# A recommender's history gather: one tile of rows in 256 moved from GpSimd to SyncE

## The chip, the cores and the metric

The kernel runs on one core of a Trainium2 chip. The metric is the device time in microseconds of one execution; for the kernel before it is a median of three executions. The engines are named as in the profile: PE (TensorE, matrix multiply), DVE (VectorE), ACT (ScalarE), POOL (GpSimd) and SP (SyncE); "SPq" is SyncE's queue of issued DMAs.

## The reference

A Deep-Interest recommender. Each of B = 16384 users has a history of L = 200 items. Every history item is looked up in an item table of V rows of D = 64 floats, compared with the candidate item, scored by a small network whose activation ("dice") is normalised over the batch, and the weighted rows are summed. Then a small three-layer head gives the output.

```python
u, it, c, h = u_emb[user], i_emb[item], c_emb[cate], i_emb[hist]     # h: (200, 16384, 64)
feat = concatenate([h, itb, h - itb, h * itb], axis=-1)              # itb: it, repeated for each l
a = dice(feat @ au_W1 + au_b1, au_alpha, axis=1)                     # mean, var over the 16384 users
cur = sum((a @ au_W2 + au_b2) * h, axis=0)
z = concatenate([u, it, c, cur], axis=-1)
z = dice(z @ W1 + b1, alpha1, axis=0); z = dice(z @ W2 + b2, alpha2, axis=0)
return z @ W3 + b3
```

So 200 x 16384, some 3.3 million, table rows are looked up by index, and that gather is most of the kernel's traffic.

## The kernel before, in words

**First stage.** The item table is copied to a table of its own in device memory (`table`), each row 2 x 64 floats (512 bytes): the item's embedding and, beside it, its product with the weights that act on the history item alone. SyncE loads blocks (L217), VectorE transposes, TensorE multiplies, ScalarE's queue stores (L232, L234). Meanwhile GpSimd gathers the user, item and category rows (24 groups of 16 gathers). `xi`, in device memory too, keeps for each of 8 chunks of users the product that belongs to the candidate item.

**The main loop.** The 16384 users are 128 partitions x 128 tiles. A *tile* is one row of `table` for each of the 128 partitions; a *step* is 16 tiles (TD), one chunk of one history position; 8 steps (ND) make a history position l, so there are 1600 steps k. A hardware loop (L411) runs 8 passes of 24 positions (192 steps), and the last 8 positions (64 steps) follow unrolled, with 10 steps to drain. The order within a step is written out by hand (`step`, L376), each engine keeps it, and an engine waits where its next instruction's data or buffer is not ready. Steps are pipelined: step k fetches k, turns k-1, ends the hidden layer of k-2 and weighs k-10.

- `fetch(k)` (L306): 16 indirect DMAs by GpSimd, one a tile (`gather`, L135, issue at L138), into `land[k % 12]`, a ring of 12 buffers; and on SyncE the load of `xit[k % 2]` from `xi` (L309).
- `load_hist_ids` (L148): on SyncE, once in 8 steps, the indices of the next history position into one of two `idx` buffers (L149); it waits for the last gather that read that buffer.
- ScalarE: the gate of k-10 (L386, L389), the copy of `xit` into `px` (L391), and, after the turn, `ph` (L393). The copy at L391 frees the `xit` buffer that SyncE waits for.
- VectorE: `turn(k-1)` (four transposes, L317, the first to wait for the gathers of k-1), the hidden layer (L329, L331), `hm` (L323), once in 8 steps the moments of the batch (L359 to L373), and `weigh(k-10)` (L337 to L353). L352 is the last to read `land[(k-10) % 12]`; a gather two steps later writes that buffer again.
- TensorE: `px` from `hm` (L176).

Completion of DMAs is counted on 8 semaphores for SyncE's and ScalarE's queues and 8 for GpSimd's, taken in turn; a DMA waits for the one eight before it. At the end of a loop pass all engines meet and the counts are set back. GpSimd goes into the first pass without waiting for SyncE; there, the ten buffers of `land` for k = -10 to -1 are set to zero by VectorE (L286) and pass through the first steps as if they had been fetched.

Of the kernel before, what the change touches and what calls it, by code (L numbers as in the profile page):

```python
# [8 lines left out]
F32 = mybir.dt.float32  # L9
I32 = mybir.dt.int32  # L10
# [4 lines left out]
P = 128  # L15
D = 64
# [3 lines left out]
CD = 2 * CH  # L20
LPB = 24
LAND = 12
EARLY = 4
IDX = 2
XI = 2
# [3 lines left out]
def din_kernel(  # L29
# [24 lines left out]
    nc = tc.nc  # L54
    L, B = r_hist.shape
    NT = B // P
    TD = 2 * CD // P
    ND = NT // TD
    V = i_emb.shape[0]
# [3 lines left out]
    const = ctx.enter_context(tc.tile_pool(name="const", bufs=1))  # L63
# [7 lines left out]
    def quarter(e, g, n=S):  # L71

        return slice((2 * e + g) * S, (2 * e + g) * S + n)
# [21 lines left out]
    for e in range(2):  # L95
        rows = au_W1.rearrange("(g d) a -> d g a", d=D)[e * S : (e + 1) * S]
        for g in range(2):
            r = quarter(e, g)
            nc.sync.dma_start(au_w[r], rows)
            for q, (a0, n) in enumerate(parts):  # L100
                c, a = quarter(q, g, n), slice(a0, a0 + n)
# [3 lines left out]
    for g in range(2):  # L105
        for q, (a0, n) in enumerate(parts):
            r, a = quarter(q, g, n), slice(a0, a0 + n)
# [12 lines left out]

    land = [const.tile([P, TD, 2 * D], F32, name=f"land{i}") for i in range(EARLY)]
    idx = [const.tile([P, NT], I32, name=f"idx{i}") for i in range(IDX)]
    stats = [const.tile([P, 2 * ND, nc.vector.BN_STATS_DIM], F32, name=f"st{i}") for i in range(2)]
    rstds = [const.tile([P, 1], F32, name=f"rs{i}") for i in range(2)]
    shifts = [const.tile([P, 1], F32, name=f"sh{i}") for i in range(2)]
# [5 lines left out]
    table = dram.tile([V, 2 * D], F32, name="table")  # L131
# [3 lines left out]
    def gather(dst, ids, rows):  # L135

        for n in range(ids.shape[1]):
            nc.gpsimd.indirect_dma_start(  # L138
                out=dst[:, n, :],
                out_offset=None,  # L140
                in_=rows,
                in_offset=bass.IndirectOffsetOnAxis(ap=ids[:, n : n + 1], axis=0),
            )
# [3 lines left out]

    def load_hist_ids(i, l):  # L148
        nc.sync.dma_start(idx[i], r_hist[ds(l, 1), :].rearrange("l (p n) -> p (l n)", n=NT))  # L149

    def by_tile(t, i):

        return t[:, ts(i, CH)].rearrange("p (n t) -> p n t", t=S)

    def transpose(dst, rows, n=TD):

        for i in range(2):
            for e in range(2):
                nc.vector.transpose(  # L159
                    by_tile(dst[ts(e, D)], i)[:, :n], rows[ts(i, D), :n, ts(e, S)]  # L160
                )
# [9 lines left out]
    def layer(dst, pairs, n=CH, onto=False):  # L171

        for i in range(2):
            cols = slice(i * CH, i * CH + n)
            for j, (lhsT, rhs) in enumerate(pairs):
                nc.tensor.matmul(  # L176
                    dst[:, cols], lhsT, rhs[:, cols],
                    start=(j == 0 and not onto), stop=(j == len(pairs) - 1),
                    skip_group_check=onto,
                )  # L180
# [13 lines left out]
    with ExitStack() as start:  # L194
# [41 lines left out]
        def fetch_one(j):  # L236
            c, k = j % ND, j // ND
            gather(land[j % EARLY][:, :, :D], ids[k][:, ts(c, TD)], (i_emb, u_emb, c_emb)[k])

        def keep_one(j):  # L240
            c, k = j % ND, j // ND
            if k == 0:
                transpose(itT[:, c], land[j % EARLY])
                layer(ph, [(blk_i, itT[:, c])])
# [3 lines left out]
            else:  # L248
                t = pre.tile([P, CD], F32, tag="t", name="t")
                transpose(t, land[j % EARLY])  # L250
                nc.scalar.dma_start(ucT[k - 1, c], t)
# [20 lines left out]
    with ExitStack() as main:  # L272
        ring = main.enter_context(tc.tile_pool(name="ring", bufs=1))

        land += [
            ring.tile([P, TD, 2 * D], F32, name=f"land{i}") for i in range(EARLY, LAND)
        ]
# [7 lines left out]
        for k in range(-10, 0):  # L285
            nc.vector.memset(land[k % LAND], 0.0)  # L286
        for t in hx:
# [7 lines left out]
        for i in range(2):  # L295
            nc.vector.memset(rstds[i], 0.0)
            nc.vector.memset(shifts[i], 0.0)
        nc.sync.dma_start(xit[-1 % XI], xi[ND - 1])

        def by_row(t):  # L300
            return t.rearrange("p (n d) -> p n d", d=D)

        def x_of(k):
            return land[k % LAND][:, :, D:]

        def fetch(k):  # L306
            l, c = divmod(k, ND)
            gather(land[k % LAND], idx[l % IDX][:, ts(c, TD)], table)
            nc.sync.dma_start(xit[k % XI], xi[c])  # L309

        def turn(k):

            rows = land[k % LAND].rearrange("p n (s e c) -> p n s e c", s=2, e=2)
            for i in range(2):
                for e in range(2):
                    dst = hx[k % 2][ts(e, D), :, ts(i, CH)]
                    nc.vector.transpose(  # L317
                        dst.rearrange("p s (n t) -> p n s t", t=S), rows[ts(i, D), :, :, e]
                    )

        def product(k):

            nc.vector.tensor_mul(hm, ph, itT[:, k % ND])  # L323
            layer(px[k % 2], [(blk_m, hm)], onto=True)

        def hidden(k):

            l, c = divmod(k, ND)
            nc.vector.tensor_add(x_of(k), by_row(px[k % 2]), by_row(hx[k % 2][:, 1]))  # L329
            for i in range(2):  # L330
                nc.vector.bn_stats(  # L331
                    stats[l % 2][:, 2 * c + i, :], x_of(k)[:, ts(i, TD // 2)]
                )

        def weigh(k):
# [14 lines left out]
            c = k % ND  # L350
            rows = land[k % LAND][:, :, :D]
            nc.vector.tensor_mul(by_row(pg), rows, w.unsqueeze(2).to_broadcast([P, TD, D]))  # L352
            nc.vector.tensor_add(cur[:, ts(c, TD)], by_row(pg), cur[:, ts(c, TD)])  # L353

        def moments(l):

            i = l % 2
            mv = small.tile([P, 2], F32, tag="mv", name="mv")
            nc.vector.bn_aggr(mv, stats[i].rearrange("p c s -> p (c s)"))  # L359
            other = small.tile([P, 2], F32, tag="other", name="other")  # L360
            for q in range(2):
                for g in range(2):
                    nc.vector.tensor_copy(other[quarter(q, g)], mv[quarter(q, 1 - g)])
            total = small.tile([P, 2], F32, tag="total", name="total")
            nc.vector.tensor_add(total, mv, other)
            mean = small.tile([P, 1], F32, tag="mean", name="mean")
            nc.vector.tensor_scalar_mul(mean, total[:, 0:1], 0.5)
            dev = small.tile([P, 1], F32, tag="dev", name="dev")
            nc.vector.tensor_sub(dev, mv[:, 0:1], mean)
            half = small.tile([P, 1], F32, tag="half", name="half")  # L370
            nc.vector.tensor_scalar_mul(half, total[:, 1:2], 0.5)
            var = small.tile([P, 1], F32, tag="var", name="var")
            nc.vector.scalar_tensor_tensor(var, dev, dev, half, ALU.mult, ALU.add)  # L373
            scale_and_shift(mean, var, P, rstds[i], shifts[i])

        def step(k, last=None):  # L376


            def has(j):
                return last is None or j <= last  # L380

            if has(k):
                fetch(k)
            if has(k - 10):
                i = (k - 10) // ND % 2
                nc.scalar.activation(  # L386
                    by_row(gate), x_of(k - 10), AF.Sigmoid, bias=shifts[i], scale=rstds[i]
                )
                nc.scalar.activation(pg, gate, AF.Identity, bias=au_al, scale=au_1al)  # L389
            if has(k - 1):  # L390
                nc.scalar.copy(px[(k - 1) % 2], xit[(k - 1) % XI])  # L391
                turn(k - 1)
                nc.scalar.copy(ph, hx[(k - 1) % 2][:, 0])  # L393
            if has(k - 2):
                hidden(k - 2)
            if has(k - 1):
                product(k - 1)
            if has(k - 2) and (k - 2) % ND == ND - 1:
                moments((k - 2) // ND)
            if has(k - 10):  # L400
                weigh(k - 10)

        def steps(l0, n, last):

            for k in range(n * ND + (10 if last else 0)):
                l, c = divmod(k, ND)
                if c == 0 and l + 1 < n + (not last):
                    load_hist_ids((l + 1) % IDX, l0 + l + 1)
                step(k, last=n * ND - 1 if last else None)

        with tc.For_i(0, L - L % LPB, LPB) as l0:  # L411
            with tc.manual_schedule():
# [5 lines left out]
    with ExitStack() as head:  # L418
# [5 lines left out]
        for g in range(2):  # L424
            t = fin.tile([P, 4, Z1], F32, name=f"w1{g}")
# [16 lines left out]
        for i, (v, n) in enumerate(((alpha1, Z1), (alpha2, Z2))):  # L442
            t = fin.tile([n, 1], F32, name=f"al{i}")
# [17 lines left out]
        for c in range(ND):  # L461
            rows = land[c % EARLY].rearrange("p (s n) d -> p s (n d)", s=2)
            for i in range(2):
# [21 lines left out]
        for m in range(2 * ND):  # L485
            a = work.tile([Z1, CD], F32, tag="a1", name="a1")
# [6 lines left out]
        for c in range(ND):  # L493
            a = work.tile([Z2, TD, 2, 2, S], F32, tag="a2", name="a2")
            for g in range(2):
                p, zm = (
                    t.rearrange("z (i n t) -> z i n t", i=2, t=S)
                    for t in dice(1, Z2, 2 * c + g, rstd, shift)
                )
# [38 lines left out]
```

## Time and profile before

| | us |
|---|---|
| median of 3 executions | 32900.87 |
| lowest, highest | 32900.82, 32961.82 |
| the profiled execution | 32903.59 |
| its span on the core | 32901.7 |
| first gather of `table` starts | 489.43 |
| second loop pass, first gather | 4338.58 |
| GpSimd busy with gathers of `table` (25600) | 24157.7 |
| VectorE busy | 25564.2 |
| ScalarE busy | 7641.4 |
| SyncE waiting for ScalarE's copy at L391 | 22516.9 |

A group of instructions is told as line, engine, operation, what is written and read, how many, then busy us and mean ns of one, then the idle time of its engine just before them and what ended most of it. "issue" is idle time in which the engine waited for nothing that the profile shows. Issuing a DMA isn't counted as busy time, but a gather on GpSimd, which is a piece of work for it, is. Times within the execution count from the start of the span.

### The profile page before, as it was taken

The numbers are of one execution on the slowest core, as the hardware profiler recorded it, in microseconds if no ns is written. First come the engines' busy times: TensorE is split into PE (matmuls) and PEld (weight loads), VectorE is DVE, ScalarE is ACT, GpSimd is POOL, SyncE is SP. The second block draws the span as 40 slices with busy tenths as digits, with TensorE's granted clock in tenths as the row PEclk, the third lists the DMA queues.
The fourth block names the chain that finished last, engine by engine and source line by source line (L and its number), as shares of the span: only waits on it lengthen the run. The fifth ranks groups of instructions, "written<-read, shape, count | busy, mean of one in ns | idle before, by whom it ended". The sixth has DMA issues, their size and how long they took to land. (4 is left out here: it accounts for less than half of the span.)

```text
span 32901.7 us, 99907 instructions
## 1 busy us (share of the span) xinstructions
PE 6388.8 (19%) x7216; PEld 2043.0 (6%) x7216; DVE 25564.2 (78%) x28837; ACT 7641.4 (23%) x7113; POOL 24520.4 (75%) x25988
## 2 busy tenths in 40 slices
PE   3111111111111111111111111111111111111113
PEld 0000000000000000000000000000000000000001
DVE  7777777777777777777777777777777777777776
ACT  1222222222222222222222222222222222222222
POOL 7777777777777777777777777777777777777774
PEclk6555555555555555555555555555555555555555
DMA  5222222222222222222222222222222222222221
GB/s 158 79 79 79 79 79 79 79 80 78 80 79 79 79 78 80 79 79 80 78 79 79 80 79 79 80 79 79 79 79 80 79 80 78 79 80 79 80 79 53
DMA packets 1208006, 2648.96 MB, mean 81 GB/s; under 512 B 549078, under 2 KB 575222, under 8 KB 1201142
## 3 DMA queue, kind: packets, MB, share of 16 engines
q0 software_dynamic: 831488, 1691.97, 19.8%
q1 hardware_dynamic: 365238, 887.18, 8.5%
q10 hardware_dynamic: 10560, 63.79, 0.5%
q14 instruction: 705, 5.78, 0.1%
q8 instruction: 15, 0.25, 0.0%
HBM read 2577.24 MB, written 63.91 MB: 80 GB/s over the span
## 5 line engine op out<-in xcount | busy, mean ns | idle before, releaser
L138 POOL DMA_INDIRECT land<-table,idx x25600 | 24157.7, 944 | 7880.7 <-issue 7560.7
L317 DVE STREAM_TRANSPOSE hx<-land 64x1024 f32<-64x1024 f32 x6404 | 7935.6, 1239 | 6418.2 <-DMA land<-table,idx 6265.7
L176 PE MATMUL px<-hm,blk_m 128*128 128x512 f32 x6404 | 5973.2, 1088 | 26045.0 <-DVE hm L323 26045.0
L389 ACT ACTIVATE pg<-gate,au_al,au_1al 128x1024 f32<-128x1024 f32 x1610 | 1943.8, 1207 | 12855.1 <-DVE cur L353 12854.8
L393 ACT COPY ph<-hx 128x1024 f32<-128x1024 f32 x1601 | 1627.7, 1017 | 10702.8 <-DVE hx L317 10702.8
L176 PEld LDWEIGHTS px<-hm,blk_m 128*128 128x128 f32 x6404 | 1878.9, 324 | 30138.6 <-DVE hm L323 28484.2
L331 DVE BATCH_NORM_STATS2 st<-land 128x6 f32<-128x512 f32 x3204 | 2060.6, 685 | 55.0
L338 DVE STREAM_TRANSPOSE yT<-pg 128x1024 f32<-128x1024 f32 x1610 | 2011.6, 1249 | 55.2
L352 DVE TENSOR_TENSOR pg<-land,ph 128x1024 f32<-128x1024 f32 x1610 | 1978.6, 1229 | 54.9
L353 DVE TENSOR_TENSOR cur<-pg,cur 128x1024 f32<-128x1024 f32 x1610 | 1971.2, 1224 | 55.6
L340 DVE TENSOR_REDUCE r<-yT 128x32 f32<-128x1024 f32 x1610 | 1964.0, 1220 | 55.3
L329 DVE TENSOR_TENSOR land<-px,hx 128x1024 f32<-128x1024 f32 x1602 | 1961.2, 1224 | 49.4
L386 ACT ACTIVATE gate<-land,sh,rs 128x1024 f32<-128x1024 f32 x1610 | 1991.7, 1237 | 2.9
L337 DVE TENSOR_TENSOR pg<-pg,land 128x1024 f32<-128x1024 f32 x1610 | 1967.5, 1222 | 10.7 <-ACT pg L389 10.7
L323 DVE TENSOR_TENSOR hm<-ph,itT 128x1024 f32<-128x1024 f32 x1601 | 1931.1, 1206 | 0.0
L391 ACT COPY px<-xit 128x1024 f32<-128x1024 f32 x1601 | 1591.4, 994 | 22.9 <-PE px L176 22.9
L347 DVE SCALAR_TENSOR_TENSOR ph<-r,au_bias,r 64x16 f32<-64x16 f32 x3220 | 770.7, 239 | 114.7
L386 ACT ACT_TABLE_LOAD x210 | 269.4, 1283 | 582.1 <-DMA land<-table,idx 372.3
L344 DVE COPY r<-r 64x32 f32<-64x32 f32 x1610 | 321.4, 200 | 55.0
L185 ACT ACT_TABLE_LOAD x203 | 260.4, 1283 | 3.6
L185 ACT ACTIVATE std<-var,eps 128x1 f32<-128x1 f32 x201 | 59.2, 295 | 716.5 <-DVE var L373 716.5
L176 PE MATMUL px<-rT,blk_h 128*128 128x512 f32 (+1 forms) x196 | 158.2, 942 | 231.1 <-DVE rT L159 231.1
(76 smaller groups left out, 1903.2 us busy)
## 6 DMA issues: line engine op xcount, KB each, us to landing
xit<-xi SPq DMA_DIRECT2D x1601, 512.0 KB, 3.9
land<-table,idx POOLq DMA_INDIRECT x25600, 2.5
table<-tab ACTq DMA_DIRECT2D x48, 1024.0 KB, 4.4
tab<-in_L_rec_i_emb SPq DMA_DIRECT2D x48, 512.0 KB, 4.3
idx<-in_r_hist SPq DMA_DIRECT2D x200, 64.0 KB, 1.8
ucT<-t ACTq DMA_DIRECT2D x16, 512.0 KB, 2.9
land<-ucT SPq DMA_DIRECT2D x16, 512.0 KB, 4.3
xi<-t ACTq DMA_DIRECT2D x8, 512.0 KB, 2.7
```

Of the source, the lines that this page charges most:

```text
L138: nc.gpsimd.indirect_dma_start(out=dst[:, n, :], out_offset=None, in_=rows, in_offset=bass.IndirectOffsetOnAxis(ap=ids[:, n : n + 1], axis=0),
L176: nc.tensor.matmul(dst[:, cols], lhsT, rhs[:, cols], start=(j == 0 and not onto), stop=(j == len(pairs) - 1), skip_group_check=onto,)
L317: nc.vector.transpose(dst.rearrange("p s (n t) -> p n s t", t=S), rows[ts(i, D), :, :, e])
L329: nc.vector.tensor_add(x_of(k), by_row(px[k % 2]), by_row(hx[k % 2][:, 1]))
L331: nc.vector.bn_stats(stats[l % 2][:, 2 * c + i, :], x_of(k)[:, ts(i, TD // 2)])
L337: nc.vector.tensor_mul(by_row(pg), by_row(pg), x_of(k))
L338: nc.vector.transpose(yT, pg)
L340: nc.vector.tensor_reduce(r, yT.rearrange("p (i n u) -> p i n u", i=2, u=S), mybir.AxisListType.X, ALU.add)
L352: nc.vector.tensor_mul(by_row(pg), rows, w.unsqueeze(2).to_broadcast([P, TD, D]))
L353: nc.vector.tensor_add(cur[:, ts(c, TD)], by_row(pg), cur[:, ts(c, TD)])
L386: nc.scalar.activation(by_row(gate), x_of(k - 10), AF.Sigmoid, bias=shifts[i], scale=rstds[i])
L389: nc.scalar.activation(pg, gate, AF.Identity, bias=au_al, scale=au_1al)
```

## The change

In every 16th step (k = 15, 31, ...; `EVERY` = 16) the last of the 16 tiles is no longer gathered by GpSimd. Its 128 rows come into a buffer of their own, `side` (two of them, used in turn), by 128 plain DMAs of 512 bytes from SyncE's queue, one for each partition, with the place in `table` in a register: 8 in each of the 16 steps before, after the step's other work is listed. For this

- `load_addresses` loads the 128 indices of the tile (one of each partition, 4 bytes each) by a SyncE DMA into one partition of `addr` (two, in turn), and VectorE multiplies them by the row's 512 bytes. It stands ahead of every step k with k % 16 = 8, for the tile after the next; in SyncE's queue it follows the idx load of that step.
- `rows_by_address` loads 8 of these addresses into SyncE's registers with one instruction, and issues 8 DMAs.
- `turn` copies `side` into the last column block of `land` on ScalarE, ahead of the transposes.
- Ahead of the loop, both `addr` are loaded, and all 128 rows of the first such tile are fetched in four parts of 32. In the built program, 4 of these DMAs stand ahead of the last xit load before the loop (L298 in the kernel before) and 124 behind it, ahead of the loop's first idx and xit loads; three of the four register loads (of 32 each) are among the 124.

The built program has 12 gathers fewer in the loop's pass (3060 for 3072) and 4 fewer after it; SyncE has 1536 row DMAs, 12 address loads and 192 register loads more in the pass.

```diff
+EVERY = 16
+ROW = 4 * 2 * D
+    side = [const.tile([P, 2 * D], F32, name=f"side{i}") for i in range(2)]
+    addr = [const.tile([1, P], I32, name=f"addr{i}") for i in range(2)]
...
+    def load_addresses(m, l):
+        t = addr[m % 2]
+        with nc.allow_non_contiguous_dma(reason="one index of each partition"):
+            nc.sync.dma_start(
+                t.unsqueeze(1), r_hist[ds(l, 1), :].rearrange("l (p n) -> l n p", p=P)[:, NT - 1 :]
+            )
+        nc.vector.tensor_scalar_mul(t, t, ROW)
+
+    def has_side(k):
+        return k % EVERY == EVERY - 1
...
+        for t in side:
+            nc.vector.memset(t, 0.0)
+        flat = table.rearrange("v d -> (v d)").bitcast(U8)
+
+        def rows_by_address(m, part, of):
+            dst = side[m % 2].bitcast(U8)
+            n = P // of
+            _, at = nc.values_load_multi_w_load_instructions(
+                addr[m % 2][:, ts(part, n)],
+                engines=(mybir.EngineType.SP,), min_val=0, max_val=ROW * (V - 1),
...
+            )
+            for j, a in enumerate(at):
+                p = part * n + j
+                nc.sync.dma_start(dst[p : p + 1], flat[ds(a, ROW)].rearrange("(o d) -> o d", o=1))
...
         def fetch(k):
             l, c = divmod(k, ND)
-            gather(land[k % LAND], idx[l % IDX][:, ts(c, TD)], table)
+            n = TD - has_side(k)
+            gather(land[k % LAND][:, :n], idx[l % IDX][:, c * TD : c * TD + n], table)
             nc.sync.dma_start(xit[k % XI], xi[c])
 
         def turn(k):
+            if has_side(k):
+                nc.scalar.copy(land[k % LAND][:, TD - 1], side[k // EVERY % 2])
...
+            end = (n if last else n + LPB) * ND
             for k in range(n * ND + (10 if last else 0)):
                 l, c = divmod(k, ND)
                 if c == 0 and l + 1 < n + (not last):
                     load_hist_ids((l + 1) % IDX, l0 + l + 1)
+                m, part = divmod(k, EVERY)
+                if part == EVERY // 2 and (m + 3) * EVERY <= end:
+                    load_addresses(m + 2, l0 + ((m + 3) * EVERY - 1) // ND)
                 step(k, last=n * ND - 1 if last else None)
+                if (m + 2) * EVERY <= end:
+                    rows_by_address(m + 1, part, EVERY)
+
+        for m in range(2):
+            load_addresses(m, ((m + 1) * EVERY - 1) // ND)
+        for part in range(4):
+            rows_by_address(0, part, 4)
```

More of the change, by code (lines that the diff above doesn't have):

```diff
@@ L22 @@
 LAND = 12
+EVERY = 16
+ROW = 4 * 2 * D
+U8 = mybir.dt.uint8
 EARLY = 4
@@ L298, in din_kernel @@
         nc.sync.dma_start(xit[-1 % XI], xi[ND - 1])
+        for t in side:
[7 more added lines that the diff above has]
+                engines=(mybir.EngineType.SP,), min_val=0, max_val=ROW * (V - 1),
+                skip_runtime_bounds_check_because="the DMA checks the address against the table",
+            )
+            for j, a in enumerate(at):
+                p = part * n + j
+                nc.sync.dma_start(dst[p : p + 1], flat[ds(a, ROW)].rearrange("(o d) -> o d", o=1))
         def by_row(t):
```

## The prediction

> **What bounds the kernel now.** I read the page's first and fifth parts, the timeline of two steps in mid-loop, and the waits.
>
> The page, busy time by engine and two of its groups of instructions (busy us, mean ns of one, then the idle time before them and its releaser):
>
> ```profile
> PE 6388.8 (19%) x7216; PEld 2043.0 (6%) x7216; DVE 25564.2 (78%) x28837; ACT 7641.4 (23%) x7113; POOL 24520.4 (75%) x25988
> ...
> L138 POOL DMA_INDIRECT land<-table,idx x25600 | 24157.7, 944 | 7880.7 <-issue 7560.7
> L317 DVE STREAM_TRANSPOSE hx<-land 64x1024 f32<-64x1024 f32 x6404 | 7935.6, 1239 | 6418.2 <-DMA land<-table,idx 6265.7
> ```
>
> VectorE has more busy time than GpSimd (78% against 75%), yet it is not the bound: before its transposes it idles 6265.7 us, about 3.9 us in each of 1600 steps, waiting for gathered rows. GpSimd waits for nobody: its idle time is "issue", 7560.7 / 25600 = 0.295 us behind every gather. The timeline of one step (start, length, engine, what, idle time before it) shows the same:
>
> ```profile
> 16013.31 0.99 ACT L391 COPY px<-xit 128x1024 f32<-128x1024 f32 x1
> ...
> 16015.01 0.94 POOL L138 DMA_INDIRECT land<-table,idx  x1 [0.30 <-issue]
> 16016.26 0.94 POOL L138 DMA_INDIRECT land<-table,idx  x1 [0.30 <-issue]
> 16016.40 5.00 DVE L317 STREAM_TRANSPOSE hx<-land 64x1024 f32<-64x1024 f32 x4 [4.32 <-DMA land<-table,idx]
> 16017.51 0.94 POOL L138 DMA_INDIRECT land<-table,idx  x1 [0.31 <-issue]
> ```
>
> One gather follows another every 1.25 us, across the border between steps too. More exactly: from 489.43 us (first gather from the table) to 4338.58 us (first of the second loop pass) lie 3072 gathers; less two stalls of 7 us (the first of them is shown below, the second is the end of the pass) that is 3835.0 / 3072 = 1.2484 us each. Sixteen make a step of 19.97 us.
>
> **What the change removes.** One gather in 256: 12 in each of 8 loop passes and 4 in the tail, so 100 of 25600. While GpSimd is the bound, each is worth a full pitch: 100 x 1.2484 = 124.8 us.
>
> A rule speaks against it: "DMA: Bandwidth & Descriptors", Rules for kernel authors, says that spreading DMAs over SP, ACT and GpSimd does not help bandwidth; all run on the same 16 engines, and only the sequencer's issue time is saved. Read alone it gives a gain of zero. The stretches (us, GpSimd's busy time in gathers, TensorE clock, DMA share, GB/s) decide which half applies:
>
> ```profile
> 20.00:480.00 460.00, 347.81 (x369) 0.65 0.71 216
> 600.00:1200.00 600.00, 453.71 (x481) 0.55 0.29 80
> ```
>
> In the loop the DMA engines are 29% busy; they aren't the limit, GpSimd's issuing is. So what the rule calls small is here the whole bound, and I take 124.8.
>
> **What it adds on SyncE, in a step.** One register load of 8 addresses and 8 DMAs of 512 bytes, after the step's xit load. SyncE's static small DMAs in the first 10 us are the nearest row for an issue:
>
> ```profile
> 3.09 0.43 SPq L108 DMA_DIRECT2D au_bias<-in_L_rec_au_b  x1
> ...
> 9.20 0.43 SPq L149 DMA_DIRECT2D idx<-in_r_hist  x1
> ```
>
> From the one to the other are 15 issues in 6.11 us: 0.41 us each. The idx load in the loop, whose address is in a register too, took 0.35. I take 0.41 a row; below is 0.35, above I allow double, 0.82, for a register-addressed row that no trace shows. No register load is in the trace. The skill's "Runtime: NRT & Kernel Launch", Instruction fetch mechanics, gives about 200 ns per register (loads from HBM; these are from SBUF), so 1.6 us for 8 as an estimate; the lower bound is nothing. Together 8 x 0.41 + 1.6 + 0.4 (xit) = 5.3 us of a 20 us step. The cover is SyncE's own waiting:
>
> ```profile
> SPq L309 <- ACT px L391: 22516.9, 1211, 25.3
> ```
>
> That is 22,517 us in which SyncE only waits for ScalarE to free an xit buffer, 14 us a step. The 9 DMAs take turns on 8 semaphores, and each waits for the one 8 back: 8 issues take 3.3 us, landing 1.8 (idx) to 3.9 us (xit), so at most half a microsecond is added. What is queued behind the rows is the next xit load; it is issued after the copy in step k-1 and needed in step k+1, 40 us on. Cost in the loop: 0. (Without the cover it would be 5 us a step, 8000 us; that is the slow rival.)
>
> **The waits it adds.** (1) Every 16 steps VectorE multiplies 128 addresses, in its order ahead of the step's transposes. The address load stands behind the idx load in SyncE's queue, and that waits for the last gather of the step before: the very moment T at which VectorE's transposes would start. So T + 0.35 + 0.4 issue + 1.8 to 3.9 landing (idx and xit bound it) + 0.15 (TENSOR_SCALAR of a column): transposes some 3.5 us late, 100 times. Covered twice: VectorE idles 4.3 us a step and catches up within the step; and GpSimd's next use of a land buffer is two steps behind its last reader (L352 ends 14.4 us after T; the gather starts 40 - 1.2 us after the same T): 24 us of slack. Cost 0; 350 us if uncovered. (2) ScalarE copies side into land before the transposes. Between a 128x1 activation (0.295 us) and the 128x1024 copy (1.02) I get 0.39 us for 128x128. It stands behind the px copy, which ended at 16014.30, 2.1 us before the transposes started: hidden; 39 us if not. After each loop pass ScalarE is behind (its px copy ended at 4342.84, the transposes began at 4337.57), so 5.6 us late eight times; the next transposes waited 6.9 us for gathers at 4360.08, which absorbs it. (3) The first row of each 16 steps waits for the side copy of the step: at T, like the idx load ahead of it. Nothing.
>
> **What it adds ahead of the loop, on the path.** All 128 rows of the first tile, in SyncE's queue ahead of the loop's first idx and xit loads. Four go out before the xit load at 496.86, hidden under the last gathers of the first stage; 124 rows and three loads of 32 registers follow it. In the kernel before:
>
> ```profile
> 496.86 0.34 SPq L298 DMA_DIRECT2D xit<-xi  x1
> 497.77 0.36 SPq L149 DMA_DIRECT2D idx<-in_r_hist  x1
> 498.18 26.70 SPq L309 DMA_DIRECT2D xit<-xi  x2
> ...
> 534.37 1.23 DVE L352 TENSOR_TENSOR pg<-land,ph 128x1024 f32<-128x1024 f32 x1
> 536.33 0.94 POOL L138 DMA_INDIRECT land<-table,idx  x1 [7.25 <-issue]
> ```
>
> GpSimd enters the loop without waiting for SyncE, gathers two steps, and at 536.33 starts the third, 0.73 us after L352 of step 0. The fourth (slot of k = 3) would start at 556.3 and needs L352 of step 1. That stands behind hm, which needs ScalarE's ph copy, behind its px copy, which needs xit(0). Now: 124 x 0.41 = 50.8 and 96 x 0.2 = 19.2, so xit(0) is issued at 498.2 + 70.0 = 568.2, lands 3.9 later at 572.1, two copies to 574.2, and from hm to GpSimd's start 10.55 us (hm 544.25, L352's end 554.07, plus 0.73): 584.7. GpSimd starts 28.4 us late. It isn't made up, since afterwards it is the bound again. By the trace's rows alone, registers free, 9 us; with rows at 0.82, 79 us. I take 28, because a register load is a round trip and the page's is the only price; the ends stay for the range.
>
> **Sum.** Profiled execution 32903.59 us (span 32901.7): - 124.8 + 28.4 + 1 (two more semaphore resets and a longer drain at 8 pass ends) = 32808.2. The median of the runs shown is 2.7 us under the profiled time: 32805.
>
> **Rivals.** What a measurement of this kernel can tell from no change is 0.2%, about 66 us: faster is under 32835, slower over 32967.
> - A longer start: rows at 0.82 us each. For it, no row of the trace is a 512-byte register-addressed load on one partition; against it, the idx load at 0.35. 32900.9 - 124.8 + 79 + 1 = 32856: within 0.2%. Chance 10%.
> - The gain is not collected: VectorE turns out to be the bound once waits (1) and (2) meet, or transposes slip. For it, VectorE is at 78%; against it, 4.3 us idle in every step. 32900. Chance 3%.
> - Slower, SyncE becomes the bound: 0.4 + 1.6 + 8r passes 19.97 us once a row takes r = 2.25 us. At 2.5 us the step is 22.0, 2.03 us longer: 1600 x 2.03 = 3250 us more, about 36,150. For it, a row waits for its semaphore's last DMA, so slow landing counts; against it, that takes a landing of 18 us. Chance 5%.
> - Slower, the added DMA traffic slows the gathers themselves: 124.8 / 25500 = 4.9 ns a gather, 0.4% of the pitch, eats the gain; 10 ns gives 25500 x 0.010 = 255 us, against a net gain of 96 (124.8 - 28.4): 32900.9 + 255 - 96 = 33,060. Against it, the gathers at 71% DMA share and those of the loop (busy us, mean ns, idle before):
>
> ```profile
> L138 POOL DMA_INDIRECT land<-in_L_rec_u_emb,ids x128 | 120.8, 943 | 39.0 <-issue 38.1 <-DMA land<-in_L_rec_u_emb,ids 0.9
> ```
>
> (120.8 + 39.0) / 128 = 1.2484 us, the loop's pitch to the nanosecond. For it, those DMAs were large, the rows are small. Chance 7%.
>
> **Numbers.** The likeliest case has 75%, own range 32782 (stall 9, a little less) to 32835. Range for 8 in 10: from 32776 (the whole 124.8, no stall) to 32865, which takes in the longer start. Faster: the likeliest case and a little of the others, 0.77; same: longer start and gain not collected, 0.13; slower: 0.10.
>
> **What would show it.** Right: gathers from the table x25500 at 944 ns with 0.295 us behind each; one GpSimd stall of some 28 us near 556 us; SyncE's row issues 0.4 us apart; VectorE's idle before the multiply some 3 us, 100 times, and less idle at the transposes; SyncE still waiting mostly for ScalarE's px copy. Wrong: GpSimd waiting for VectorE in mid-loop, a pitch above 1.2484, ScalarE's px copy waiting for xit, or a start stall of more than 80 us.

## The result and the profile after

| | before | after |
|---|---|---|
| median of 6 runs, us | 32901.04 | 32777.92 |
| lowest, highest | 32900.74, 32961.82 | 32776.65, 32778.23 |
| profiled execution, us | 32903.59 | 32777.75 |
| its span | 32901.7 | 32775.9 |

The ratio is 0.9962, with a 95% interval of 0.9952 to 0.9972: the changed kernel is 123 us, or 0.38%, faster. The forecast was 32805, so the direction held and 27 us of the gain were not foreseen. No chip is on record for these runs; as the kernel before took 32901.04 us beside them, they are counted with the first of the two chips named below (32900.75).

The page of the changed kernel, busy time by engine and the same two groups as before (busy us, mean ns of one, idle time before them and its releaser):

```profile
PE 6395.0 (20%) x7216; PEld 2044.0 (6%) x7216; DVE 25619.7 (78%) x28939; ACT 7665.2 (23%) x7214; POOL 24422.0 (75%) x25888
...
L144 POOL DMA_INDIRECT land<-table,idx x25500 | 24059.4, 944 | 7852.3 <-issue 7532.9
L354 DVE STREAM_TRANSPOSE hx<-land 64x1024 f32<-64x1024 f32 x6404 | 7938.0, 1240 | 5528.1 <-DMA land<-table,idx 5338.6
```

GpSimd has 100 gathers fewer, each still 944 ns with "issue" behind it, so in the loop it is still the engine that waits for nobody. VectorE's idle time ahead of the transposes fell from 6265.7 to 5338.6 us.

The waits of the changed kernel (engine and line, what it waited for, us in total, times, longest) show where SyncE and VectorE stand:

```profile
SPq L344 <- ACT px L428: 17754.3, 1201, 24.1
```

```profile
DVE hx L354 <- DMA land<-table,idx: 5338.6, 1447, 6.5
DVE addr L164 <- DMA addr<-in_r_hist: 702.6, 98, 8.2
DVE hx L354 <- ACT land L349: 115.0, 9, 15.4
```

SyncE still waits mostly for ScalarE's copy of `xit`, 17,754 us for 22,517 before. The new wait of VectorE at the multiply of the addresses (L164) is there, 7.2 us each time. The step around one of them, in VectorE's timeline:

```profile
667.48 0.39 DVE L164 TENSOR_SCALAR addr<-addr 1x128 int32<-1x128 int32 x1 [7.27 <-DMA addr<-in_r_hist]
667.88 5.00 DVE L354 STREAM_TRANSPOSE hx<-land 64x1024 f32<-64x1024 f32 x4
685.16 5.00 DVE L354 STREAM_TRANSPOSE hx<-land 64x1024 f32<-64x1024 f32 x4 [1.63 <-DMA land<-table,idx]
```

The transposes behind the multiply start late, and those of the next step wait for gathers again (1.63 us): VectorE has caught up within one step.

The start of the loop, in the timelines of SyncE and of GpSimd (start, length, engine, what, idle before it):

```profile
496.97 48.66 SPq L332 DMA_DIRECT2D side<-table  x124
546.22 0.37 SPq L155 DMA_DIRECT2D idx<-in_r_hist  x1
546.64 0.42 SPq L344 DMA_DIRECT2D xit<-xi  x1
```

```profile
538.91 0.94 POOL L144 DMA_INDIRECT land<-table,idx  x1 [9.98 <-issue]
563.27 0.94 POOL L144 DMA_INDIRECT land<-table,idx  x1 [4.70 <-issue]
```

The 124 rows and their three register loads keep SyncE for 48.66 us, and `xit(0)` is issued at 546.64. GpSimd's stall before its third step grew from 7.25 to 9.98 us, and a second stall of 4.70 (0.30 is the usual gap) stands before the fourth. Together the start costs 9.98 + 4.70 - 7.25 - 0.30 = 7.1 us.

The ends of the loop passes moved as well. The first gathers of the second and third pass, before and after:

```profile
4338.58 0.94 POOL L138 DMA_INDIRECT land<-table,idx  x1 [7.43 <-issue]
8184.13 0.94 POOL L138 DMA_INDIRECT land<-table,idx  x1 [10.69 <-issue]
```

```profile
4329.35 0.94 POOL L144 DMA_INDIRECT land<-table,idx  x1 [6.53 <-issue]
8158.63 0.94 POOL L144 DMA_INDIRECT land<-table,idx  x1 [9.79 <-issue]
```

Each stall is 0.9 us shorter: seven of these, and 0.14 at the last border, make 6.4 us. So the difference adds up as - 124.8 (gathers) + 7.1 (start) - 6.4 (pass ends) = -124.1 us, where the two profiled executions differ by 125.8 and the medians by 123.1.

### The profile page after: what moved, and what is told of

The parts are those of the page before. It is cut to its first block, busy times and chain, and to the rows that moved or that the text cites. A ratio compares the mean times of both kernels' runs of the same rounds, so it can differ in the third digit from the quotient of the medians.

```text
span 32775.9 us, 127799 instructions
## 1 busy us (share of the span) xinstructions
PE 6395.0 (20%) x7216; PEld 2044.0 (6%) x7216; DVE 25619.7 (78%) x28939; ACT 7665.2 (23%) x7214; POOL 24422.0 (75%) x25888
## 5 line engine op out<-in xcount | busy, mean ns | idle before, releaser
L354 DVE STREAM_TRANSPOSE hx<-land 64x1024 f32<-64x1024 f32 x6404 | 7938.0, 1240 | 5528.1 <-DMA land<-table,idx 5338.6
L164 DVE TENSOR_SCALAR addr<-addr 1x128 int32<-1x128 int32 x100 | 31.2, 312 | 702.6 <-DMA addr<-in_r_hist 702.6
```

The source lines that it names most:

```text
L354: nc.vector.transpose(dst.rearrange("p s (n t) -> p n s t", t=S), rows[ts(i, D), :, :, e])
```

## The experiments

My theory: GpSimd's issue of gathers is the bound, SyncE's new work is hidden in its waits for ScalarE, and only the start costs time. The rivals are that the small DMAs slow the gathers, that VectorE's new waits cost something, and that SyncE becomes the bound.

The first four kernels ran on one chip, where the kernel before took 32900.75 us (median of 16 runs).

**Removal alone.** The gathers are left out and nothing takes their place: no address loads, no row DMAs, no side copy. The 16th tile's rows in those steps are whatever the buffer held, so a part of the computation is left out.

```diff
-            if has_side(k):
-                nc.scalar.copy(land[k % LAND][:, TD - 1], side[k // EVERY % 2])
...
-                    load_addresses(m + 2, l0 + ((m + 3) * EVERY - 1) // ND)
+                    pass
...
-                    rows_by_address(m + 1, part, EVERY)
+                    pass
-
-        for m in range(2):
-            load_addresses(m, ((m + 1) * EVERY - 1) // ND)
-        for part in range(4):
-            rows_by_address(0, part, 4)
+
```

> The removal alone: the 16th tile of every 16th step is left out and what lay in its place is used; no addresses, no rows, no copy of side. Theory A (GpSimd's issuing is the bound, each gather is worth one pitch): 32901.0 - 100 x 1.2484 = 32776.2, and the start as in the kernel before, one stall of 7.3 us. The ends of the passes decide a second point: if their stall is 0.9 us shorter because of the missing gather in the last step, it is 32770; if SyncE's added work in the changed kernel shortened it, 10.7 us stay and it is 32776. Rival B (the added DMAs make the gathers faster or slower): the pitch here differs from the changed kernel's 1.2483 us by more than 1 ns, and the time by more than 25 us from 32770 to 32776.

Measured: 32769.2 us (32768.28 to 32777.88), ratio 0.996 (0.9946 to 0.9974). That is 131.6 us less than before, while 100 gathers are 124.8. The rest is at the pass ends, in GpSimd's timeline of this kernel:

```profile
536.44 0.94 POOL L144 DMA_INDIRECT land<-table,idx  x1 [7.30 <-issue]
...
8153.33 0.94 POOL L144 DMA_INDIRECT land<-table,idx  x1 [9.71 <-issue]
```

The start is that of the kernel before (7.30 against 7.25, no second stall), and the pass-end stall is 9.71 where it was 10.69. So the shorter pass ends belong to the missing gathers, not to SyncE's new work. (The traced execution took 32777.88 us, 8.7 over the median: its 25500 gathers are busy 24070.0 us, 10.6 more than in the changed kernel's trace, some 0.4 ns each. So single stalls are read from the traces here, and totals from the medians.) All that is added then costs 32777.92 - 32769.2 = 8.7 us across the two groups of runs.

**The additions alone.** GpSimd gathers all 16 tiles, and everything added stays.

```diff
-            n = TD - has_side(k)
+            n = TD
```

> The addition alone: all that SyncE, VectorE and ScalarE do more stays, and GpSimd gathers all 16 tiles in every step (the copy of side writes the same rows once more). Theory A (the additions lie beside GpSimd's gathers; only the start costs, 2.7 + 4.4 us): 32901.0 + 7.1 = 32908, or 32902 if the shorter pass ends belong to SyncE's work. The gathers' pitch stays 1.2484. Rival B (small DMAs slow the gathers): each ns is 26 us, so 5 ns gives 33036. Rival C (the waits of VectorE and ScalarE reach GpSimd when the gathers are not fewer): up to 350 us more, 33250, and GpSimd waiting for VectorE in mid-loop.

Measured: 32909.46 us (32908.4 to 32919.47), ratio 1.0003 (0.9993 to 1.0012): 8.7 us more than before. The start is most of it, 11.09 + 4.34 - 7.25 - 0.30 = 7.9 us. This kernel's gathers (page) and stalls (timeline):

```profile
L144 POOL DMA_INDIRECT land<-table,idx x25600 | 24163.8, 944 | 7888.7 <-issue 7638.9
```

```profile
540.31 0.95 POOL L144 DMA_INDIRECT land<-table,idx  x1 [11.09 <-issue]
564.32 0.95 POOL L144 DMA_INDIRECT land<-table,idx  x1 [4.34 <-issue]
```

A gather takes 944 ns beside the small DMAs as it does without them; the means of all these traces lie within 0.5 ns. This rules out, on this chip, the rival that the small DMAs slow the gathers, which needed 4.9 ns or more on each. The pass-end stalls were 7.51 and 10.77, 0.08 longer than before: that is the size of what SyncE's additions cost there.

**The first tile by one gather.** The 128 rows ahead of the loop are fetched by GpSimd in one gather, so 128 row DMAs and four register loads are gone from SyncE's queue. The computation is complete.

```diff
-        for m in range(2):
-            load_addresses(m, ((m + 1) * EVERY - 1) // ND)
-        for part in range(4):
-            rows_by_address(0, part, 4)
+        first = const.tile([P, 1], I32, name="first")
+        with nc.allow_non_contiguous_dma(reason="one index of each partition"):
+            nc.sync.dma_start(
+                first, r_hist[ds((EVERY - 1) // ND, 1), :].rearrange("l (p n) -> p (l n)", n=NT)[:, NT - 1 :]
+            )
+        gather(side[0].unsqueeze(1), first, table)
+        load_addresses(1, (2 * EVERY - 1) // ND)
```

> The 128 rows ahead of the loop are fetched by one gather of GpSimd in place of 128 row DMAs of SyncE; the loop is unchanged. Theory A (they delayed the first xit load of the loop, and with it GpSimd by 4.4 us): the stall at 563 us is gone, one gather more: 32778 - 4.4 + 1.2 = 32775. The other 2.7 us (the first stall is 10.0 us where it was 7.3) stay, since they come from the copy of side that the first transposes wait for. Rival (the start is made up later anyway): 32778 + 1.2 = 32779.

Measured: 32772.22 us (32771.31 to 32773.66), ratio 0.9961 (0.9947 to 0.9975), 5.7 us under the changed kernel and the lowest time of a complete computation here. The second stall is gone, and the first is the only one at the start:

```profile
524.15 0.29 ACT L349 COPY land<-side 128x128 f32<-128x128 f32 x1
524.48 5.00 DVE L354 STREAM_TRANSPOSE hx<-land 64x1024 f32<-64x1024 f32 x4 [2.82 <-ACT land L349]
...
539.63 0.94 POOL L144 DMA_INDIRECT land<-table,idx  x1 [9.22 <-issue]
```

So the second stall was SyncE's 124 rows. What is left of the first, 9.22 against 7.25, is the side copy: the first transposes wait for it, as it stands behind ScalarE's copy of `xit`. The gain is larger than the 3 us expected: the pass-end stalls are shorter too, 9.44 us where the changed kernel has 9.79, some 2.3 us in all, and why is not known.

**The addresses loaded one step later.** The load then isn't in the queue behind the idx load, and the multiply doesn't stand where VectorE waits.

```diff
-                if part == EVERY // 2 and (m + 3) * EVERY <= end:
+                if part == EVERY // 2 + 1 and (m + 3) * EVERY <= end:
```

> The address load one step later (ninth of each 16), so that it no longer stands behind the idx load, which waits for the gathers. Theory A (VectorE's 702 us of waiting for addresses are covered by its idle time): VectorE's wait before the multiply falls from 702 us to less than 100, the transposes wait about 700 us longer for gathers instead, and the time stays 32778 within 2 us. Rival C (the wait reaches GpSimd through late land buffers): the time falls by up to 350 us, at the least by 20.

Measured: 32779.01 us (32777.87 to 32779.43), ratio 0.9963 (0.9949 to 0.9977). In this kernel's trace no wait of VectorE at L164 is left, 702.6 us in the changed kernel, and the time is not lower. The wait was covered, as forecast: VectorE waits for gathers instead, 5980.4 us at its transposes where it was 5338.6:

```profile
DVE hx L354 <- DMA land<-table,idx: 5980.4, 1470, 6.5
```

**A larger share for SyncE.** One tile in 8, in 4 and in 2, so 16, 32 and 64 rows in each step, and one in 4 with the first tile by a gather. What is changed is `EVERY` and the column of the indices; for one in 2, two calls of the rows a step.

```diff
-EVERY = 16
+EVERY = 8
...
+        at = (((m + 1) * EVERY - 1) % ND + 1) * TD - 1
...
-                t.unsqueeze(1), r_hist[ds(l, 1), :].rearrange("l (p n) -> l n p", p=P)[:, NT - 1 :]
+                t.unsqueeze(1), r_hist[ds(l, 1), :].rearrange("l (p n) -> l n p", p=P)[:, at : at + 1]
```

> One tile in every 8 steps instead of 16: 16 row DMAs a step, 200 gathers fewer than before. Theory A: 100 gathers more are removed than in the changed kernel, at 1.2484 us, and SyncE's step (some 0.4 + 1.2 + 16 x 0.35 = 7.2 us) stays beside the gathers: 32778 - 124.8 = 32653. Rival (VectorE's added waits begin to count): between 32653 and 32778.

> One tile in every 4 steps: 32 row DMAs a step, 400 gathers fewer. Theory A: 32778 - 300 x 1.2484 = 32403; SyncE's step is some 0.4 + 2 + 32 x 0.35 = 13.6 us, below the gathers' 15.75 x 1.2484 = 19.7 us. Rival: a row costs more when 32 follow each other (semaphores of 8 before), SyncE's step passes 19.7 us from 0.54 us a row, and the time is above 32450.

> One tile in every 2 steps: 64 row DMAs and two register loads of 32 a step, 800 gathers fewer. Theory A: the slow rival of the prediction becomes true here, SyncE is the bound: 0.4 + 2 x 1.8 + 64 x 0.35 = 26.4 us a step, 1600 x 26.4 + 900 around the loop = 43,100, within 1500; SyncE waits no more for ScalarE's copy of px, GpSimd waits for VectorE, and it for xit. If rows were issued faster than 0.23 us each, GpSimd would stay the bound: 32778 - 700 x 1.2484 = 31904.

> One tile in every 4 steps, and the first 128 rows by one gather ahead of the loop. Theory A: both gains add: 32403 - 5.7 (as the run with the first rows by a gather showed: 32772.2 against 32777.9) = 32398, the fastest of all.

These four ran on another chip, and there the kernel before itself took 36931.6 us (36919.75 to 36935.29), 12% more than on the first. The ratios are to that:

| one tile in | us | ratio | 95% interval |
|---|---|---|---|
| 8 | 40571.95 | 1.0994 | 1.0976 to 1.1012 |
| 4 | 49909.29 | 1.3515 | 1.3492 to 1.3537 |
| 2 | 65896.89 | 1.7844 | 1.7815 to 1.7874 |
| 4, first by a gather | 49900.69 | 1.3513 | 1.3491 to 1.3536 |

All four expectations failed, the first two and the last by their sign. The third had SyncE as the bound, as it came about, but at 43,100 us. The page of the kernel with one tile in 4 shows a bound that has moved, and its waits show to where:

```profile
L144 POOL DMA_INDIRECT land<-table,idx x25200 | 23774.7, 943 | 25179.3 <-issue 24727.5
...
L165 DVE TENSOR_SCALAR addr<-addr 1x128 int32<-1x128 int32 x400 | 85.9, 215 | 20490.8 <-DMA addr<-in_r_hist 20490.8
...
L429 ACT COPY px<-xit 128x1024 f32<-128x1024 f32 x1601 | 1601.1, 1000 | 15114.8 <-DMA xit<-xi 15071.1
```

```profile
SPq L345 <- ACT px L429: 19.0, 7, 11.0
```

A gather takes what it took, 943 ns, but GpSimd idles 25,179 us around them. VectorE waits 20,491 us for addresses and ScalarE 15,071 us for `xit`, both of which come from SyncE. SyncE, which waited 17,754 us for ScalarE in the changed kernel on the first chip, waits 19. Now it is the bound. With one tile in 8, too, it waits for ScalarE for only 1126.1 of 40566.6 us. Two neighbouring stretches show what it does. SyncE's row DMAs, 32 in each, then GpSimd's gathers in the same stretches (us, GpSimd's busy time and number, TensorE clock, DMA share, GB/s), and the gather that ends GpSimd's pause:

```profile
10047.43 60.74 SPq L333 DMA_DIRECT2D side<-table  x32
...
10110.79 10.29 SPq L333 DMA_DIRECT2D side<-table  x32
```

```profile
10050.00:10108.00 58.00, 34.56 (x37) 0.52 0.15 43
10110.00:10135.00 25.00, 0.00 (x0) 0.50 0.12 37
```

```profile
10139.10 0.94 POOL L144 DMA_INDIRECT land<-table,idx  x1 [43.57 <-issue]
```

32 rows take 10.29 us (0.32 each, as on the first chip) while GpSimd stands still, and 60.74 in a stretch in which it gathers for the first 48 us (until 10095.5, by the idle time before the gather at 10139.10); SyncE stays slow for some 10 us after that. In the single records of the slow stretch (each row DMA comes with a register move), the first 39 instructions of SyncE follow each other in 52.5 us, 1.35 us each; their lengths and the gaps between them are nearly all close to 0, 0.70 or 1.40 us. The whole loop agrees. From 600 to 30000 us of this kernel's trace, row DMAs start 1.46 us apart in the mean while GpSimd gathers, and 0.45 once it has stood still for 12 us; with one tile in 8 it is 1.75 and 0.42 (distances over 5 us left out). Gathering alone doesn't do it: in the changed kernel, counted with the first chip, it is 0.39, no row DMA took longer than 0.314 us and no register move longer than 0.042, with GpSimd gathering nearly all the time. These answers for the rows of the changed kernel and for those of one tile in 8 (ns, least, median and most) show it:

```profile
L332 SPq MOVE side<-table x12800: 29/29/42, 481.5 to 32048.4; - x197
L332 SPq DMA_DIRECT2D side<-table x12800: 222/228/314, 481.5 to 32048.5; - x197
```

```profile
L333 SPq MOVE side<-table x25600: 1/29/1422, 583.1 to 40051.6; - x199
L333 SPq DMA_DIRECT2D side<-table x25600: 1/228/1407, 583.1 to 40051.7; - x199
```

What follows is limited. These runs show what the kernel looks like when SyncE is the bound, and that a share of one in 8 is enough for that on this second chip. They don't show where the limit lies on the first chip, since the larger shares have not been run there. They don't tell either what the changed kernel does on the second chip: it has not been run there, and there is no trace of the kernel before from it. An estimate from the trace with one tile in 8: at its mean beside gathers, 1.75 us a row, 8 rows take 14.0 us, and at 2.06 (a slow stretch of 32.90 us for 16 rows) 16.5, of a step that is 36931.6 / 1600 = 23.1 us there. That leaves room, but not much, and nothing here measures it.

Why SyncE's instructions are slow on that chip, and whether that also makes the kernel before 12% slower, stays open. Two things narrow it. The row DMAs aren't needed for the chip to be slower: in the kernel with one tile in 4 the first gather of `table` starts at 583.03 us, 0.8 us after the first row, where the changed kernel has 489.24. And the gathers aren't slower: where they follow each other there, it is 0.94 us and a gap of 0.30 as on the first chip, so 25600 of them would take 25600 x 1.2484 = 31,959 us. By this estimate GpSimd waits in the kernel before on that chip, and a gather less need not be worth its pitch there.

## Why the prediction was right, and where it was off

- *What bounds the kernel.* Right. Removing 100 gathers and adding nothing gives 131.6 us, 124.8 of them as 100 x 1.2484. The rule of the Trainium skill, "DMA: Bandwidth & Descriptors", Rules for kernel authors, that spreading DMAs over engines doesn't help bandwidth but only saves issue time, was read rightly: what was saved is issue time, 124.8 us of it on the engine that sets the pace.
- *SyncE's work in the loop costs nothing.* Right on the first chip, but for 0.08 us at each pass end. It does not slow the gathers (944 ns with all additions, 944 without), and SyncE keeps 17,754 us of waiting. 8 rows took 2.85 us in a mid-loop step, 0.36 each.
- *The waits added.* Right. The multiply waits 7.2 us where VectorE idled 4.3 before, so it comes about 3 us late; with the multiply's 0.39 the transposes are some 3.4 us late, 3.5 as forecast; taking the wait away changes nothing. The side copy was put behind the px copy and called hidden, which holds in mid-loop: of the nine waits (115.0 us), one is at the start and eight at the first step behind a pass border. These eight were forecast, 5.6 us late and absorbed; at the second pass the transposes started 4.47 us after its first gather where it was 1.01 ahead of it, so 5.5 late, and no stall of GpSimd follows. At the start it doesn't hold: the first transposes wait 2.31 us for it, since the px copy there comes late. This was missed. It is not in the sum twice, because the wait for `xit(0)` that follows ends later anyway.
- *The start: the mis-sized term.* Forecast 28.4 us, measured 7.1. The mechanism and its chain were right, and two prices in it were not. The forecast took 124 x 0.41 + 96 x 0.2 = 70.0 us for SyncE; it was 48.66. In the records, the three loads of 32 registers took 2.13 us each, 6.4 together and not 19.2; what remains, 42.3 us, is 0.34 a row and not 0.41. With 48.7 in place of 70.0, from where the rows start, the prediction's chain gives 496.97 + 48.7 + 1.0 (idx load and gaps) = 546.6 for `xit(0)`, + 3.9 + 2.1 + 10.55 = 563.2 for the stalled gather. It started at 563.27. The larger part of the error, 12.8 of 21 us, is the register load: the Trainium skill's "Runtime: NRT & Kernel Launch", section Instruction fetch mechanics, gives about 200 ns a register. That is for loads from device memory; from on-chip memory a load of 8 took 0.718 us here and one of 32 took 2.13, so 67 to 90 ns a register, and the measurement decides. The lower end that the prediction had worked out, registers free and a stall of 9 us, was nearer.
- *Pass ends.* Forecast + 1 us. The additions did cost 0.08 us at each of them, some 0.6 in all, but the missing gathers took 0.98 off each, 6.4 us net. The prediction had no term for this. Why the stall at the pass end is shorter behind 15 gathers than behind 16 was not tried and stays open.
- *The rivals.* Not the longer start (a row costs 0.34, not 0.82), not the gain uncollected, not slower gathers. The one that SyncE becomes the bound did not come about in the changed kernel on the first chip. But such a price was met: on the second chip, rows beside gathers came 1.46 and 1.75 us apart in the mean (one tile in 4 and in 8), 1.9 and 2.06 in slow stretches. That is under the 2.25 at which 8 rows a step decide, though not by much, and above the 1.1 or so at which 16 do ((19.97 - 2.0) / 16).

The two terms that were off, 21 us at the start and 7 at the pass ends, both made the kernel faster than forecast; they are about the 27 us by which the forecast was high. The measured 32777.92 lies under the range given to the likeliest case (32782 to 32835) and 2 us inside the outer one (32776 to 32865), whose low end meant no stall at all. The stall did come; that the time is as if it hadn't is luck, since the unpriced gain at the pass ends, 6.4 us, nearly cancels the 7.1 at the start. With + 1 at the pass ends, as forecast, it would be 32901.0 - 124.8 + 7.1 + 1 = 32784, inside the likeliest case.

## What to carry to other kernels

Where one engine issues without ever waiting, a piece of its work was worth its whole pitch here (gap included, 1.2484 and not 0.944 us), and handing it to a queue that mostly waits was free in the loop; check then what that queue does ahead of the loop, where nothing covers it. There one gather of 1.25 us for the first tile was better than 128 DMAs, by 5.7 us. A margin that rests on the idle time of another engine should be read as a price per instruction at which it is gone. Here a row beside gathers cost 0.39 us on one chip, and 1.46 or 1.75 with larger shares on another.

## What was unexpected of the hardware

- A register load by SyncE grows slowly with the number of registers: 0.718 us for 8 and 2.13 for 32, which gives 0.25 us plus 0.059 a register; for 16 that is 1.19, and the median with one tile in 8, on the second chip, is 1.16.
- On the second chip, SyncE's row DMAs came 1.46 us apart in the mean while GpSimd gathered and 0.45 when it had stood still (one tile in 4), and 32 rows took 60.74 us in place of 10.29, although the gathers themselves took 943 ns as on the first. The kernel before took 36931.6 us there and 32900.75 on the first.
